# Moving the pieces of a projection to fixed steps in a graph attention kernel, and its first weights ahead of other work

## The chip, the cores and the metric

The kernel runs on one core of a Trainium2 chip. The metric is the device time of one execution in microseconds (us). The median of several runs counts, and a profile of one further execution tells where its time goes.

## What is computed

The program is a graph layer with attention, a graph convolution and two layer norms. Nearly all of its time goes into the attention, which is this part of the reference:

```python
q = (x @ Wq.T).reshape(d, n, h)
k = (x @ Wk.T).reshape(d, n, h)
v = (x @ Wv.T).reshape(d, n, h)
a = jnp.einsum('dnh,dmh->dnm', q, k) * scale
a = a + spatial_encoding + edge_encoding
a = jax.nn.softmax(a, axis=2)
out = jnp.einsum('dnm,dmh->dnh', a, v)
```

Here n = 2708, d = 128 and h = 8, and both encodings are the adjacency matrix `adj` (2708 x 2708). So there are 128 attention problems of 2708 x 2708 scores. All of them add the same matrix `adj` twice before the exponential. The reshape takes the projected rows in their flat order: problem d uses the values from d x 2708 x 8 on, which belong to a short run of rows of x. The projections of later rows of x are therefore needed only by later problems.

## The kernel before, in words

**Tiles.** Four problems make a group (`GB = 4`), so there are 32 groups. The 2708 queries of a group are cut into six blocks of 452 (the last has 448), and the 2708 keys into 21 chunks of 128 and a short one of 20. A block is worked through in nine steps, which gives 54 steps in a group and 1728 in all. A step takes two to four *pieces* of the scores, of two tiles of 128 keys x 452 queries each (tile `s` in PSUM, two buffers), and three more tiles of the chunk that the step treats in another way (tile `p` in PSUM, one buffer).

**One step on each engine.** TensorE makes the scores (L438). VectorE adds the adjacency to the two tiles of a piece and writes them to `e` (L445). ScalarE takes the exponential of the three tiles in `p` and writes `w` (L534), and GpSimd multiplies `w` with the exponential of the adjacency (L535). When all pieces of the step have been added, ScalarE takes the exponential of `e` in one instruction (L537). Later TensorE multiplies the weights in `e` and `w` with the values and adds up in `acc` (L455, L460, L463). At the end of a block VectorE copies `acc` out (L469). In the first group ScalarE also makes the exponentials of the adjacency (L418), which are stored to memory (L420) and read back in the later groups.

**The order of TensorE's work** is made by the generator `interleave` (L40 to L129) when the program is built. It keeps estimates of when each engine will be done, and yields one of four things: a piece of scores, an addition to `acc` (`add_up`), the copy of a finished block (`hand_on`), or a piece of a projection (`amid`). Each engine gets its instructions in the order in which the generator yields them. A projection piece comes ahead of the step's first piece of scores, and at which steps one comes is told by the list `amid` (L474). The assertion below that list holds a projection to being done before its group needs it.

**The projections.** The projections of the first two chunks of 128 rows of x are made whole, ahead of the attention (`project_all`, L377 to L406). Those of the other 20 chunks are cut into 240 pieces, 12 to a chunk: K, Q and V, four pieces each (`quarters`, L321). These are the pieces that the list `amid` places. One piece (`project`, L338) is a product of 128 rows with 256 columns of weights (L344, two instructions on TensorE, which use one of the two `s` buffers), a copy by VectorE (L346), for K and Q a split into two parts on GpSimd (L359, L360), two stores (L364), or one for V (L354), and the load of the next piece's weights (`load_quarter`, L329, with the DMA in L336). The copy goes with the product. The split, the stores and the load are put on the list `jobs`, and one job is taken from it in each step, ahead of its second piece of scores (L495): the split in the step of the projection, the stores in the next, the load in the one after that. For V the store comes in the same step and the load in the next. The tiles for the weights (`wc`), for the rows of x (`xc`) and for the copies have one buffer each.

**The DMA queue of SyncE (SP).** SP issues nearly all DMAs, in program order. At the start of a step it gets the loads of adjacency tiles for the steps ahead (`load_adj`, eight tiles ahead, L513), in the fourth step of a block those of the next queries (L500), and over a group those of the next group's keys and values (L505 to L511). Before the attention starts it gets, in this order: x and the weights for the first two chunks (L370, L373), two adjacency tiles (L375), the stores of the first chunk's K and Q, the loads of the first group's keys and queries, six more adjacency tiles, the values, the stores of the second chunk, and then the rows and weights for the first piece (`load_quarter(0)`, L407).

The functions around the change, with the lines that the profile names:

Of the kernel before, what the change touches and what calls it, by code (L numbers as in the profile page):

```python
# [142 lines left out]
def graph_attention_gcn(ctx: ExitStack, tc: tile.TileContext, x, xT, adj, adjT, adjP, adjS,  # L143
# [45 lines left out]
    with ExitStack() as s:  # L189
# [28 lines left out]
        for m in range(NU):  # L218
            if m not in TWO_EXP:
                pairs += [[(m, 0), (m, 1)], [(m, 2), (m, 3)]]  # L220
            elif left_over.index(m) % 2:
# [4 lines left out]
        plan = [(pairs[cuts[i] : cuts[i + 1]], m, [j for j in range(GB) if j != left_out[m]])  # L226
                for i, m in enumerate(TWO_EXP)]
# [62 lines left out]
        def load_adj(n):  # L290
            g, b, m = loads[n]
            n0, nw = QBS[b]
            if isinstance(m, tuple):
                t = adj_cols[g, b, m] = twos.tile([P, 2, QB], F32, tag="two", name="two")
                for i, x in enumerate(m):
                    nc.sync.dma_start(t[:, i, :nw], (adjS if x == NU else adjP[ds(x * P, P), :])[:, ds(n0, nw)])
            elif m < 0 and g > 0:
                t = exp_cols[g, b, -1 - m] = ecols.tile([P, QB], F32, tag="ecol", name="ecol")
                nc.sync.dma_start(t[:, :nw], near_exp[b, -1 - m][:, :nw])
            else:  # L300
                t = adj_cols[g, b, m] = cols.tile([P, QB], F32, tag="col", name="col")
                m = -1 - m if m < 0 else m
                nc.sync.dma_start(t[:, :nw], adjP[ds(m * P, P), ds(n0, nw)])
# [17 lines left out]
        quarters = [(c, i, h) for c in range(FIRST, NM) for i in range(3) for h in range(4)]  # L321
# [7 lines left out]
        def load_quarter(n):  # L329
            c, i, h = quarters[n]  # L330
            i0, mi = MC[c]
            if i == h == 0:
                given[c] = proj.tile([P, P], F32, tag="xc", name="xc")
                nc.sync.dma_start(given[c][:, :mi], xT[:, ds(i0, mi)])
            given[c, i, h] = proj.tile([P, QW], F32, tag="wc", name="wc")
            nc.sync.dma_start(given[c, i, h], projections[i][0][:, ts(h, QW)])  # L336
# [36 lines left out]
            nc.sync.dma_start(first_w[:, ds(2 * NB * i, 2 * NB)], w)  # L373
        for n in range(2):
            load_adj(n)  # L375

        def project_all(c, i):  # L377

            dst = projections[i][1]
            pp = ps.tile([P, 2, NB], F32, tag="s", name="s")  # L380
            for h in range(2):
                nc.tensor.matmul(pp[:, h, :], first_x[:, ts(c, P)], first_w[:, ts(2 * i + h, NB)], start=True, stop=True)
            o = flat(epool.tile([P, 8, QB], F32, tag="e", name="e"))[:, : 4 * NB].rearrange("p (l f) -> p l f", l=2)
            if i == 2:
                nc.scalar.copy(o[:, 0], flat(pp))
                return lambda: nc.sync.dma_start(dst.rearrange("(i g) e -> i (g e)", g=P)[ts(c, P)], o[:, 0])
            f = half_scale if i == 1 else 1.0
            nc.scalar.mul(o[:, 0].bitcast(F32R), flat(pp), f)
            nc.vector.scalar_tensor_tensor(o[:, 1].bitcast(F32R), flat(pp), f, o[:, 0], ALU.mult, ALU.subtract)
            return lambda: nc.sync.dma_start(dst.rearrange("r (i g) -> i r g", g=P)[ts(c, P)],  # L390
                                             o.rearrange("p l (e g) -> p (l e) g", g=P))
# [12 lines left out]
            load_values(0, j)  # L404
        for i in range(3):
            project_all(1, i)()  # L406
        load_quarter(0)  # L407
        for h in range(9):
            order_keys(0, h, (nc.gpsimd.tensor_copy, nc.vector.tensor_copy, nc.scalar.copy)[h % 3])
        for j in range(GB):  # L410
# [60 lines left out]
                nc.sync.dma_start(os_[:, ds((GB * g + j) * N + n0, nw)], o[ds(32 * j, H + 1), :nw])  # L471

        where = {}
        amid = [2 + 32 * n // 5 for n in range(len(quarters))]  # L474
        for g in range(1, NG):
            c = (min(NG, g + 2) * GB * N - 1) // (P * P)
            assert c < FIRST or amid[quarters.index((c, 2, 3))] + 8 < 54 * g
# [375 lines left out]
```

## Time and profile before

| what | value |
|---|---|
| median of 3 runs | 6884.85 us (6881.82 to 6886.79) |
| the profiled execution's own time | 6884.26 us |
| its span in the profile | 6882.5 us |
| ScalarE, exponential of `e` (L537) | 1728 instructions, mean 2658 ns |
| ScalarE, exponential of `w` (L534) | 1728 instructions, mean 1323 ns |
| VectorE, addition of adjacency (L445) | 5568 instructions, mean 1.09 us |
| GpSimd, product (L535) | 1728 instructions, mean 3102 ns |
| projection piece on TensorE (L344) | 480 instructions, mean 428 ns |
| projection piece on VectorE (L346) | 240 instructions, mean 418 ns |
| projection piece on GpSimd (L359, L360) | 160 each, about 402 and 736 ns |
| DMA | 1674 MB, mean 243 GB/s |

The profile is of one execution. Times in it are counted from the start of its span, and its span is 1.8 us shorter than the execution's own time. A row of the waits view names an engine and line, what ended its wait, the total in us, how often, and the longest. A row of the timeline has the start and the length in us, the engine, the line, the operation, the tiles it writes and reads, and how many like instructions were put together in it (`x2`). In square brackets stands how long the engine had been idle and what ended that. Durations of instructions that follow each other on one engine may overlap in the record.

### The profile page before, as it was taken

What the parts mean: (1) busy time and instruction counts of PE and PEld (TensorE: products, weight loads), DVE (VectorE), ACT (ScalarE), POOL (GpSimd) and SP (SyncE); (2) the same over time, 40 slices, a digit from 0 to 9 for tenths busy, and PEclk for the clock granted to TensorE, in tenths of its full rate; (3) what the DMA queues carried; (4) which work ended last, traced back from release to release, by engine and by line L of the source; (5) the groups of instructions that cost most, each with busy time, mean ns of one, the idle gap of its engine ahead of it and who ended that gap; (6) DMA issues with size and microseconds to landing.
All of it is one profiled execution on the core that took longest, in us unless ns stands there. A gap on an engine that the chain in (4) does not pass through costs nothing.

```text
span 6882.5 us, 138849 instructions
## 1 busy us (share of the span) xinstructions
PE 6655.3 (97%) x50666; PEld 2002.7 (29%) x50666; DVE 6106.7 (89%) x6373; ACT 6505.4 (95%) x3659; POOL 5789.3 (84%) x2706
## 2 busy tenths in 40 slices
PE   7999999999999999999999999999999999999979
PEld 2222222222222222222222222222222222222254
DVE  6899999999999999999999999999999999999941
ACT  7999999999999999999999999999999999999910
POOL 5899988989888899998889999889898898888800
PEclk8999999999999999999999999999999999999999
DMA  8888888778888877788887778887788878777667
GB/s 254 261 250 250 249 244 248 243 246 250 249 254 245 239 245 244 246 251 252 246 243 248 244 240 250 242 253 243 248 251 247 249 233 239 243 233 230 193 204 233
DMA packets 1168590, 1674.27 MB, mean 243 GB/s; under 512 B 153982, under 2 KB 1135954, under 8 KB 1163802
## 3 DMA queue, kind: packets, MB, share of 16 engines
q1 hardware_dynamic: 1167642, 1664.50, 79.0%
q8 instruction: 402, 6.59, 0.4%
q14 instruction: 290, 2.38, 0.1%
q10 hardware_dynamic: 256, 0.81, 0.1%
HBM read 1582.90 MB, written 81.80 MB: 242 GB/s over the span
## 4 chain that ended last, share of the span: by engine, by line
PE 58%; DMA 11%; DVE 11%; POOL 6%; issue 5%; ACT 5%; SPq 4%; DVEq 0%; ACTq 0%; POOLq 0%
PE acc L463 29%; PE s L438 18%; DVE e L445 10%; POOL w L535 6%; DMA col<-in_adjP 4%; PE acc L680 3%; DMA two<-in_adjP 3%; ACT e L537 3%; PE p L438 2%; PE acc L455 2%; SPq L287 2%; ACT w L534 2%; DMA ecol<-ne 2%; PE s L344 1%; PE acc L460 1%
## 5 line engine op out<-in xcount | busy, mean ns | idle before, releaser
L535 POOL TENSOR_TENSOR w<-w,ecol 128x1356 f32<-128x1356 f32 (+1 forms) x1728 | 5347.8, 3102 | 696.1 <-ACT w L534 601.6
L445 DVE TENSOR_TENSOR e<-s,col 128x904 f32<-128x904 f32 (+1 forms) x4608 | 4817.2, 1091 | 320.6 <-PE s L438 130.3
L537 ACT ACTIVATE e<-e 128x2712 f32<-128x2712 f32 (+5 forms) x1728 | 4593.8, 2658 | 9.3 <-DVE e L445 4.3
L463 PE MATMUL acc<-e,vals 128*9 128x452 f32 x20352 | 3561.9, 545 | 0.4 <-ACT e L537 0.4
L438 PE MATMUL s<-q,k 32*128 32x452 f32 x10944 | 2475.2, 462 | 120.9 <-DVE e L445 93.3
L534 ACT ACTIVATE w<-p 128x1356 f32<-128x1356 f32 (+1 forms) x1728 | 2286.0, 1323 | 33.9 <-PE p L438 20.4
L438 PEld LDWEIGHTS s<-q,k 32*128 32x128 f32 x10944 | 997.6, 182 | 3267.6 <-DVE e L445 2845.5
L463 PE MATMUL acc<-w,vals 128*9 128x452 f32 x10368 | 1622.0, 544 | 0.0
L438 PE MATMUL p<-q,k 32*128 32x452 f32 (+1 forms) x5184 | 1328.1, 444 | 21.2 <-ACT w L534 19.6
L445 DVE TENSOR_TENSOR e<-s,two 128x904 f32<-128x904 f32 (+1 forms) x960 | 1048.3, 1092 | 126.5 <-PE s L438 81.3
L463 PEld LDWEIGHTS acc<-e,vals 128*9 128x9 f32 x20352 | 441.7, 88 | 786.2 <-issue 773.7
L438 PEld LDWEIGHTS p<-q,k 32*128 32x128 f32 x5184 | 547.1, 182 | 51.0 <-ACT w L534 45.3
L463 PEld LDWEIGHTS acc<-w,vals 128*9 128x9 f32 x10368 | 207.0, 88 | 175.8 <-issue 160.3
L262 POOL CAST k<-k_raw 128x336 fp32r<-128x336 f32 x251 | 222.2, 886 | 30.1 <-DMA q<-qs 30.1
L460 PE MATMUL acc<-e,v_first 128*32 128x452 f32 (+1 forms) x1536 | 188.9, 564 | 9.8 <-DVE o L469 2.0
L455 PE MATMUL acc<-e,v_short 128*128 128x452 f32 (+1 forms) x384 | 195.1, 590 | 0.0
L344 PE MATMUL s<-wc,xc 128*128 128x256 f32 (+1 forms) x480 | 166.4, 428 | 8.9 <-DMA wc<-in_WkT 7.5
L469 DVE COPY o<-acc 128x452 f32<-128x452 f32 x192 | 119.9, 624 | 40.0 <-PE acc L463 39.8
L360 POOL TENSOR_TENSOR pr<-pa,pr 128x256 fp32r<-128x256 f32 (+1 forms) x160 | 117.8, 736 | 12.8
L346 DVE TENSOR_SCALAR pa<-s 128x256 f32<-128x256 f32 (+1 forms) x240 | 100.2, 418 | 27.6 <-PE s L344 23.9
L344 PEld LDWEIGHTS s<-wc,xc 128*128 128x128 f32 (+1 forms) x480 | 70.5, 184 | 133.4 <-DVE e L445 116.4
L680 PE MATMUL acc<-col,xw 128*128 128x512 f32 (+2 forms) x264 | 106.0, 551 | 0.0
(85 smaller groups left out, 1041.6 us busy)
## 6 DMA issues: line engine op xcount, KB each, us to landing
col<-in_adjP SPq DMA_DIRECT2D x1965, 226.0 KB
two<-in_adjP SPq DMA_DIRECT2D x1440, 226.0 KB
ecol<-ne SPq DMA_DIRECT2D x1395, 226.0 KB
col<-in_adjP SPq DMA_DIRECT2D x393, 224.0 KB
two<-in_adjP SPq DMA_DIRECT2D x288, 224.0 KB
ecol<-ne SPq DMA_DIRECT2D x279, 224.0 KB
col<-in_adjT SPq DMA_DIRECT2D x210, 256.0 KB
k_raw<-ks SPq DMA_DIRECT2D x504, 84.6 KB
```

Source lines behind the costliest of these rows:

```text
L262: copy(k[:, :, ts(i, n)], t[:, ts(i, n * NU)].rearrange("p (q c) -> p c q", c=NU))
L287: queues[i].dma_start(q[ds(32 * j + 2 * H * i, 2 * H), :nw].bitcast(F32), qs[:, ds((GB * g + j) * N + n0, nw)])
L344: nc.tensor.matmul(pp[:mi, 0, :QW], given[c][:, :mi], given.pop((c, i, h)), start=True, stop=True)
L438: nc.tensor.matmul(to[:, :nw], k[r, m, :], q[r], start=True, stop=True)
L445: nc.vector.tensor_add(e[:, ds(at, 2), :nw], st[:, :, :nw], a)
L455: nc.tensor.matmul(a[:, :nw], vz, e[:, t, :nw], start=False, stop=False)
L460: nc.tensor.matmul(a[ds(32 * j, 32), :nw], v_first[g % 2][:, ds(32 * j, 32)], e[:, t, :nw], start=True, stop=False)
L463: nc.tensor.matmul(a[ds(32 * j, VW), :nw], v[:, m, ds(VW * j, VW)], e[:, t, :nw], start=False, stop=(m == last_chunk))
L534: nc.scalar.activation(w[:, :, :nw], sp[:, :, :nw], AF.Exp, scale=2.0)
L535: nc.gpsimd.tensor_mul(w[:, :, :nw], w[:, :, :nw], exp_cols[g, b, two][:, :nw].unsqueeze(1).to_broadcast([P, 3, nw]))
L537: nc.scalar.activation(e[:, :at, :nw], e[:, :at, :nw], AF.Exp, scale=2.0)
L680: nc.tensor.matmul(acc[:, :nw], src[:mw, m, :], t[:mw, :nw], start=(m == 0), stop=(last is None and m == NM - 1))
```

## The change

The first piece's rows and weights are loaded right behind the first two adjacency tiles, no longer behind the work on the second chunk. The list of the steps that a projection piece is put in front of is another one. Before, piece n (from 0) stood in front of step 2 + 32n // 5, that is one in 6.4 steps, at changing steps of a block. Now three pieces stand in every 18 steps (two blocks), always in front of steps 1 and 8 of the first block and of step 4 of the second. The pattern begins with its second place: the first piece stands in front of step 8, the next ones in front of steps 13, 19, 26, 31 and so on. The last piece, which stood in front of step 1531, now stands in front of step 1441. The number of pieces and what each does stay the same.

```diff
         for n in range(2):
             load_adj(n)
+        load_quarter(0)
 
         def project_all(c, i):
...
         for i in range(3):
             project_all(1, i)()
-        load_quarter(0)
         for h in range(9):
...
         where = {}
-        amid = [2 + 32 * n // 5 for n in range(len(quarters))]
+
+        assert len(plan) == 9
+        amid = [18 * (n // 3) + (1, 8, 13)[n % 3] for n in range(1, len(quarters) + 1)]
         for g in range(1, NG):
```

## What was predicted, and from what

> **What bounds the kernel now.** I read the page's busy times first.
>
> ```profile
> PE 6655.3 (97%) x50666; PEld 2002.7 (29%) x50666; DVE 6106.7 (89%) x6373; ACT 6505.4 (95%) x3659; POOL 5789.3 (84%) x2706
> ```
>
> TensorE looks busiest, but its matmuls overlap in the record, so I asked which engine never rests while the attention runs. It runs from about 44 to 6540 us, and ScalarE's exponentials (L534 on the product scores `w`, L537 on the added scores `e`) are due once in each of its 1728 steps. ScalarE's waits from 244 to 5840 us, where pieces of projections (L344) stand between the steps, are:
>
> ```profile
> ACT w L534 <- PE p L438: 17.6, 40, 0.8
> ACT e L537 <- DVE e L445: 3.3, 12, 0.6
> ACT w L534 <- PE s L438: 1.2, 4, 0.4
> ACT w L534 <- POOL w L535: 0.8, 1, 0.8
> ```
>
> That is 22.9 us of rest in 5596 us: ScalarE is the bound, and the other engines' waits are slack. An edit that leaves ScalarE's work alone can only win back its delays. To size them I read the timeline of ScalarE at the first L534 of groups 1, 27, 28 and 31 (54 steps a group; the last piece stands before step 1531, group 28).
>
> ```profile
> 283.10 1.36 ACT L534 ACTIVATE w<-p 128x1356 f32<-128x1356 f32 x1
> ...
> 5529.98 1.29 ACT L534 ACTIVATE w<-p 128x1356 f32<-128x1356 f32 x1
> ...
> 5731.72 1.30 ACT L534 ACTIVATE w<-p 128x1356 f32<-128x1356 f32 x1 [0.73 <-PE p L438]
> ...
> 6332.94 1.29 ACT L534 ACTIVATE w<-p 128x1356 f32<-128x1356 f32 x1
> ```
>
> A group with pieces takes (5529.98 - 283.10)/26 = 201.80 us, one without (almost) (6332.94 - 5731.72)/3 = 200.41. The pieces cost 1.40 us a group, 0.166 us for each of some 8.44. So all of them together cost about 38 us; that is what a better place can win at most, apart from the start. At the start the timeline shows this:
>
> ```profile
> 49.34 1.18 SPq L334 DMA_DIRECT2D xc<-in_xT  x1
> 50.57 1.24 SPq L336 DMA_DIRECT2D wc<-in_WkT  x1
> ...
> 53.28 0.19 ACT L418 ACTIVATION_READ_ACCUMULATOR ecol<-col 128x1 f32 x1
> ...
> 54.91 1.19 PE L344 MATMUL s<-wc,xc 128*128 128x256 f32 x2 [7.48 <-DMA wc<-in_WkT]
> ...
> 61.45 1.30 ACT L534 ACTIVATE w<-p 128x1356 f32<-128x1356 f32 x1 [7.98 <-PE s L438]
> ```
>
> The first piece stands before step 2; TensorE waits 7.48 us for its weights, and ScalarE, which needs step 2's scores from behind it, stands still for 7.98 us.
>
> **What the Trainium skill says.** "Perfetto Trace Analysis", Identifying the Most-Contended Engine, says that occupancy names the contended engine, except that matmul occupancy does not; the trace agrees, with ScalarE at rest for 0.4% of the middle. The same page, Optimizing Scalar/DVE Operations, says that half of a ScalarE instruction's own overhead, in the record, overlaps the next one; here L534 lasts 1.30 us and the next L537 starts 1.18 us after it. So I count from start to start. "PSUM — Partial Sum Buffer", Engine vs sequencer instructions, says that matmuls keep program order and the other queues are strict FIFO; the stall above agrees: what stands behind the piece waited 7.5 us with it. "DMA: Bandwidth & Descriptors", Anatomy of one DMA, says that waits are made by the issuing sequencer and prices a transfer at 2.0 us + bytes/436e3, for the 131 KB of weights an estimate of 2.3 us; here it was 4.3 us (50.57 to 54.88), behind three stores. I use 4.3.
>
> **The change part by part.** Nothing is added or removed: 240 pieces before and after, each two PE instructions, one DVE copy, two POOL instructions (not for V), its stores and one load. SP's queue has as many rows. What changes is where they stand.
>
> (1) *The first load, ahead of the second chunk's work.* SP issues xc and wc behind the adjacency loads, after 3.8 us; SP has nothing to issue from there to 11.19, so they cost nothing there. Every DMA waits for the one eight places before it on its semaphore; two more loads use two more of the eight, but those that come around have landed, and the key reads keep their pace. Behind the second chunk's stores two issues fall away, and the loads for steps 3 and 4 move ahead from 51.98 to 49.34, by 2.6 us.
>
> (2) *The first piece goes from step 2 to step 8*, for which the weights are there. Step 2's scores then need the p bank, free at 51.31 when L534 of step 1 ends (50.03 + 1.28); an e buffer, free when the store issued at 44.00 has been read (the same store at 11.19 had landed by 16.50, so 5.3 us, 49.3); and adjacency loaded long before. So ScalarE goes on at 53.47: up to 7.98 us won. What is late next is step 3's adjacency: issued until about 51.0 and landed by 55.3 (with 4.3 us), while the last add of step 3 has to start by 57.7 (L534 and L537 of step 2 and L418 and L534 of step 3 from 53.47 make 58.8, less 1.09 for the add). That fits by 2.4 us, on transfers that are busy with the stores. The piece's other instructions (VectorE's copy 0.42, POOL's 1.14, two stores and the next load on SP) leave steps 2 to 4 for steps 8 to 10, where the places of (3) price them. Bounds 5.0 and 8.0; I take 7.5.
>
> (3) *The places after that.* I write a piece's place as its step in the block of 9. Before, 2 + 6.4n (rounded down) visits all nine evenly. For each step I took the time from its L534 to the next step's L534 over what is usual for this step of the block (its 30th percentile, so the noise floor is near nothing), and summed over a piece's six steps, from the one before it to four after. Mean over 25 or 26 pieces at places 0 to 8: 0.55, 0.02, 0.02, 0.25, 0.26, 0.16, 0.22, 0.39, 0.39 us; mean 0.25. The new places 1, 8, 4 look like (0.02 + 0.39 + 0.26)/3 = 0.22, little better. But the planner also orders the work around a piece, so I ran its plain Python for both lists and took the order alone, no time, from it. After, the order repeats every 18 steps. Of these, 16 have steps in the trace before with the same order from two steps ahead to three behind (11 to 31 cases each), and the other two (next block, steps 1 and 2) over a narrower stretch. Their mean delays, summed: the piece at place 8 costs 0.39 (0.37 of it at the next block's first step, which has four adds), the one at place 4, in its new order, 0.09 and 0.06 at step 7, the one at place 1 0.01, the rest 0.02: 0.57 us in 18 steps. The trace shows the two costly ones:
>
> ```profile
> 4076.22 0.41 DVE L346 TENSOR_SCALAR pa<-s 128x256 f32<-128x256 f32 x1
> 4077.42 2.10 DVE L445 TENSOR_TENSOR e<-s,col 128x904 f32<-128x904 f32 x2 [0.79 <-ACT w L534]
> ...
> 4083.40 1.36 ACT L534 ACTIVATE w<-p 128x1344 f32<-128x1344 f32 x1
> 4084.93 3.19 ACT L537 ACTIVATE e<-e 128x3584 f32<-128x3584 f32 x1 [0.17 <-DVE e L445]
> ```
>
> Place 8: VectorE copies the piece, stands still, then adds without rest, and is late at the block's first step: L537 starts 1.53 us after L534, not 1.18.
>
> ```profile
> 3622.86 0.70 PE L344 MATMUL s<-wc,xc 128*128 128x256 f32 x2
> ...
> 3628.84 2.50 ACT L537 ACTIVATE e<-e 128x2712 f32<-128x2712 f32 x1
> 3631.27 1.30 ACT L534 ACTIVATE w<-p 128x1356 f32<-128x1356 f32 x1
> ```
>
> Place 4: the next L534 starts 2.43 us after L537, not 2.35. Filling every step from 54 to 1673 in this way gives 47.6 us of delay after; the same steps had 60.2 before (2.1 a group; 0.75 where no piece stands). Won: 12.6 us. The bound from below is places 8 and 4 at their plain means, (0.02 + 0.39 + 0.26) + 0.03 = 0.70 a period, 0.13 more in 77 periods, 10 us: 2.6 won. From above, if the stall at place 8 was only half as long, 80 x 0.19 = 15 more: 27. Likely 9 to 16.
>
> (4) *The queues passed.* SP: the weights for the piece at place 4 are issued two steps after the piece at place 8 and are due three steps later. Before, the 27 such loads were issued 4.1 us ahead of that step's L534 in the median (0.6 behind it at worst) and landed 3.8 us later; they are due 5.05 us behind it. Cover: 5.3 us; a gap of five steps instead of six eats 3.5 of what there was. POOL: a split (0.40 + 0.74) now falls on fixed steps of the group, some beside the key copies (0.89); POOL's product ended at most 6.8 us after its L534's start, against 4.5 usual, and is added up later than that. Both at nothing.
>
> **Sum.** From the profiled execution's own 6884.26 us (span 6882.5 and 1.8 around it; the median of the runs is 6884.85): 6884.26 - 7.5 - 12.6 = 6864.2 us.
>
> **Rivals.** 0.2%, 13.8 us, is about what a measurement of this kernel can tell from no change: 6871.1 to 6898.6 counts as the same.
> *B, the start gives nothing:* behind the stores the transfers are the bound, and ScalarE waits at steps 3 to 5 instead of step 2. For it: the issues of SP at 44 to 52 us are slow (1.2 to 3.1 us). Against it: 2.4 us of slack and far more bytes an us later. Then 6884.26 - 12.6 = 6871.7.
> *C, slower, the weights at place 4 late:* if SP is as late at that load as it is before step 3 of a block (3.4 us behind L534), they land at 3.4 + 3.8 = 7.2, and are due at 5.05: TensorE waits 2.2 us in each of 80 periods, all of it on ScalarE: 6864 + 172 = 7036. It decides from a lateness of 1.2 us on. Against it: none of the 27 was so late.
> *D, more won:* the piece at place 8 always stands seven steps behind the one before it, so VectorE may have recovered and the delay may go: 80 x 0.39 = 31 less, 6833. Against it: the 20 like cases cost 0.26 to 0.75 each.
>
> **Chances.** Forecast 0.80, B 0.10, C 0.05, D 0.05. The forecast alone spans 6857 (start 8.0, places 19) to 6871, and the range goes to 6873 to hold B. Faster by over 0.2%: 0.84 (D, and nearly all of the forecast); within: 0.11; slower: 0.05.
>
> **What would show it.** Right: no L344 row before 60 us and L534 of step 2 at about 53.5 without idle time; ScalarE's first L534 of groups 1 and 27 about 201.4 us a group apart (199.66 without any delay, and three times 0.57); the delays at the first step of every second block, about 0.37 us each. Wrong: ScalarE waiting for adjacency or adds between 55 and 70 us (2); PE L344 idle before it on DMA wc (4); delays at other steps of the 18 (3).

## The result, and the profile after

The changed kernel takes 6870.08 us (median of 16 runs, 6864.01 to 6881.51) against 6886.35 before (16 runs). The ratio is 0.9977, with a 95% interval of 0.9970 to 0.9984: some 16 us faster, between 11 and 21. The forecast was 20 us, 6864.2. The profiled execution took 6865.95 us, with a span of 6863.4.

The page's busy times of the changed kernel:

```profile
PE 6632.4 (97%) x50666; PEld 1992.4 (29%) x50666; DVE 6109.7 (89%) x6373; ACT 6506.3 (95%) x3659; POOL 5788.8 (84%) x2706
```

The instruction counts are those of before, and the busy times of ScalarE (ACT), VectorE (DVE) and GpSimd (POOL) are the same to within 0.1%. So no work of these engines went; only waiting did. L534 and L537 of before are L536 and L539 now. These are all of ScalarE's waits in the changed kernel from 240 to 5840 us:

```profile
ACT e L539 <- DVE e L445: 11.1, 25, 0.7
ACT w L536 <- PE p L438: 1.0, 3, 0.3
```

It was 22.9 us in 57 waits, most of them on the product scores `p`. Now it is 12.1 us, nearly all on VectorE's adds. The first exponentials of groups 1, 27 and 31 in ScalarE's timeline give the time of a group:

```profile
276.75 1.50 ACT L536 ACTIVATE w<-p 128x1356 f32<-128x1356 f32 x1
...
5514.81 1.45 ACT L536 ACTIVATE w<-p 128x1356 f32<-128x1356 f32 x1
...
6317.17 1.29 ACT L536 ACTIVATE w<-p 128x1356 f32<-128x1356 f32 x1
```

(5514.81 - 276.75)/26 = 201.46 us a group, where it was 201.80; the four groups from 27 on, which have no pieces, take (6317.17 - 5514.81)/4 = 200.59. I took each step's delay as in the prediction, against the same usual times. It makes 50.7 us from step 54 to 1673, where it was 60.2.

**Where the 19.1 us between the two spans came from:** 6.3 us up to group 1's first exponential (283.10 to 276.75), 9.4 in steps 54 to 1673 and 4.5 in the last steps (7.5 to 3.0 us of delay), less 1.2 lost in the layers behind. Not all of this belongs to the change. Of the 6.3, 1.6 lie ahead of the first exponential, whose time varied between 39.7 and 46.5 us in the profiles below. The last steps cost 5.8 to 7.7 us in eleven of the twelve. One profile is one execution, and its parts have to be read next to those of other kernels with the same stretch.

### The profile page after: what moved, and what is told of

Read it like the earlier page. It is cut to its first block, busy times and chain, and to the rows that moved or that the text cites. A ratio compares the mean times of both kernels' runs of the same rounds, so it can differ in the third digit from the quotient of the medians.

```text
span 6863.4 us, 138873 instructions
## 1 busy us (share of the span) xinstructions
PE 6632.4 (97%) x50666; PEld 1992.4 (29%) x50666; DVE 6109.7 (89%) x6373; ACT 6506.3 (95%) x3659; POOL 5788.8 (84%) x2706
## 4 chain that ended last, share of the span: by engine, by line
PE 52%; DMA 12%; DVE 11%; POOL 7%; issue 7%; ACT 6%; SPq 5%; DVEq 0%; POOLq 0%; ACTq 0%
PE acc L463 26%; PE s L438 16%; DVE e L445 9%; POOL w L537 6%; DMA col<-in_adjP 4%; DMA two<-in_adjP 3%; SPq L287 3%; PE acc L682 3%; ACT e L539 3%; ACT w L536 2%; DMA ecol<-ne 2%; PE acc L455 2%; PE p L438 2%; PE s L344 1%; DMA two<-in_adjS 1%
## 5 line engine op out<-in xcount | busy, mean ns | idle before, releaser
L537 POOL TENSOR_TENSOR w<-w,ecol 128x1356 f32<-128x1356 f32 (+1 forms) x1728 | 5347.5, 3102 | 678.8 <-ACT w L536 598.4
L539 ACT ACTIVATE e<-e 128x2712 f32<-128x2712 f32 (+5 forms) x1728 | 4616.5, 2672 | 17.6 <-DVE e L445 12.0
L536 ACT ACTIVATE w<-p 128x1356 f32<-128x1356 f32 (+1 forms) x1728 | 2308.2, 1336 | 3.0 <-PE p L438 2.5
```

The source lines that it names most:

```text
L536: nc.scalar.activation(w[:, :, :nw], sp[:, :, :nw], AF.Exp, scale=2.0)
L537: nc.gpsimd.tensor_mul(w[:, :, :nw], w[:, :, :nw], exp_cols[g, b, two][:, :nw].unsqueeze(1).to_broadcast([P, 3, nw]))
L539: nc.scalar.activation(e[:, :at, :nw], e[:, :at, :nw], AF.Exp, scale=2.0)
```

## Experiments

Twelve kernels ran. Each ratio is against the kernel before on the same chip; the changed kernel's is 0.9977. In the diffs `-` is the changed kernel unless another is named.

### Which part of the change does it: the load, the places, the start

*The load alone* (the changed kernel with the old list):

```diff
-        amid = [18 * (n // 3) + (1, 8, 13)[n % 3] for n in range(1, len(quarters) + 1)]
+        amid = [2 + 32 * n // 5 for n in range(len(quarters))]
```

> The first piece's weights are loaded ahead of the second chunk's work, the pieces stay at their old steps (the first at step 2). Theory: the change wins 6 us at the start, where TensorE no longer waits for weights, and 9 us by the places after that; so this kernel wins about 6 us, 6880 against 6886 before, and ScalarE's delays in groups 1 to 29 stay at 60 us. Rival 1, the start makes all of it: 6870. Rival 2, the places make all of it: 6886.

Measured: 6886.44 us, ratio 0.9999 (0.9991 to 1.0007). The load alone wins nothing that can be told. TensorE's wait for weights is gone, but ScalarE's 8 us of rest at step 2 come back in parts over steps 1 to 8. All stalls in the first 12 steps make 8.2 us here, 9.2 before. The delay of steps 54 to 1673 is 4.7 us above that of before, with the same list; two profiles can lie that far apart.

*The places alone* (the kernel before with the new list):

```diff
-        amid = [2 + 32 * n // 5 for n in range(len(quarters))]
+        amid = [18 * (n // 3) + (1, 8, 13)[n % 3] for n in range(1, len(quarters) + 1)]
```

> The new places, with the first piece's weights loaded where they were, behind the second chunk's stores. Theory: the places win their 9 us; at the start step 2 no longer waits, but the loads for steps 3 to 5 stand behind the two extra issues (2.4 us), so only 3 to 4 us are won there: 6873. Rival 1, the early load makes all of it: 6886. Rival 2, the places make all of it and the load's place is worth nothing: 6870.

Measured: 6866.43 us, ratio 0.9976 (0.9969 to 0.9982). That is the whole effect, as rival 2 had it. The profile has 44.5 us of delay in steps 54 to 1673.

*The new start with the old rest:*

```diff
         amid = [18 * (n // 3) + (1, 8, 13)[n % 3] for n in range(1, len(quarters) + 1)]
+        amid[15:] = [2 + 32 * n // 5 for n in range(15, len(quarters))]
```

> Early load, the first 15 pieces at the new places and the other 225 at the old ones. Theory: the start's 6 us and some 0.6 us for group 1, nothing after that: 6879, with ScalarE's delays in groups 2 to 29 as before (58 us). Rival, the gain is in the start alone: 6870.

Measured: 6883.74 us, ratio 0.9999 (0.9991 to 1.0007), and 59.0 us of delay. Load and first piece together are worth about 2 us by the medians, which this measurement can't tell from nothing; its interval reaches to 6 us won, not to 7.5. The first 12 steps' stalls are 6.9 us. The theory's 6 us at the start fell here.

### What took the start's gain

In the changed kernel, step 2 no longer waits, as predicted. Here are ScalarE's exponentials of `w` in steps 2 and 3, and the exponential of adjacency that opens step 5:

```profile
52.00 1.30 ACT L536 ACTIVATE w<-p 128x1356 f32<-128x1356 f32 x1 [0.15 <-PE s L438]
...
56.47 1.28 ACT L536 ACTIVATE w<-p 128x1356 f32<-128x1356 f32 x1
...
66.51 0.58 ACT L418 ACTIVATE ecol<-col 128x452 f32<-128x452 f32 x1 [2.29 <-DMA col<-in_adjP]
```

And this is SP's timeline ahead of that wait:

```profile
58.72 5.04 SPq L287 DMA_DIRECT2D q<-qs  x8
63.86 0.37 SPq L303 DMA_DIRECT2D col<-in_adjP  x1
```

The adjacency for step 5 is issued behind eight loads of queries, which hold SP for 5 us. Before, TensorE's 7.5 us of waiting had hidden them. To see whether SP's order or the transfers are the bound, I issued these queries later:

```diff
-                if i == 3 and nq[0] < NG:
+                if i == (3 if n > 9 else 7) and nq[0] < NG:
```

> The changed kernel, in which the loads of the second block's queries, in the first block alone, are issued in step 7 and not in step 3. Theory: of the 9.4 us won at step 2 the profile shows 3 given back at steps 3 to 6, where ScalarE waits for adjacency that SP issued behind eight loads of queries (5 us of SP); without them there the start wins 2 to 3 us more: 6867. Rival, the transfers and not SP's order are the bound there: 6870, with the wait at step 5 as it is.

Measured: 6867.93 us, ratio 0.9969 (0.9958 to 0.9979). The interval overlaps the changed kernel's, so a gain in time isn't shown. That the wait at step 5 goes is shown: the same exponential starts without one.

```profile
59.31 0.58 ACT L418 ACTIVATE ecol<-col 128x452 f32<-128x452 f32 x1 [1.19 <-DMA col<-in_adjP]
...
65.42 1.30 ACT L536 ACTIVATE w<-p 128x1356 f32<-128x1356 f32 x1 [1.32 <-PE s L438]
...
68.98 0.58 ACT L418 ACTIVATE ecol<-col 128x452 f32<-128x452 f32 x1
```

What stays are 1.2 us at step 3, on adjacency, and 1.3 at step 4. So the queries in front of step 5's tiles cost what stood there; the rest is left to the transfers behind the second chunk's stores, which was not tested by itself. The stalls of the first 12 steps are 4.5 us with this edit. With the changed kernel's start as it is they were 4.8, 6.9, 8.0 and 6.5 us in four profiles (the changed kernel, the new start with the old rest, and the two with the copy twice, below), 6.5 in the mean, with 0.7 to 2.3 us of waiting at step 5. But over all 54 steps of the first group the delay is 36.7 us, and 34.6, 36.9, 37.8 and 36.5 in those four (30.5 of each are the extra exponentials): what the edit wins by step 12 it loses again by step 54.

### What a piece in front of step 8 costs, and why

Mean delay of ScalarE at some of the 18 steps (us), from groups 1 to 25. The steps are counted from 0; the pieces stand in front of steps 1, 8 and 13, and steps 9 and 13 are the first and the fifth of the second block. "The planner" is the generator `interleave`.

| kernel | step 1 | step 9 | step 13 | all 18 |
|---|---|---|---|---|
| changed | 0.01 | 0.38 | 0.09 | 0.62 |
| VectorE's copy twice at step 8 | 0.01 | 0.36 | 0.08 | 0.58 |
| VectorE's copy twice at step 1 | 0.20 | 0.45 | 0.10 | 0.87 |
| no engine's work in any piece | 0.00 | 0.29 | 0.00 | 0.44 |
| planner not told of step 8 | 0.01 | 0.06 | 0.59 | 0.81 |
| the same, no engine's work at step 8 | 0.00 | 0.00 | 0.02 | 0.20 |

*VectorE's copy twice*, in front of step 8 and, in another kernel, of step 1 (with `== 1`):

```diff
-            nc.vector.tensor_scalar_mul(a, pp[:mi, 0, :QW], half_scale if i == 1 else 1.0)
+            for _ in range(2 if amid[n] % 9 == 8 else 1):
+                nc.vector.tensor_scalar_mul(a, pp[:mi, 0, :QW], half_scale if i == 1 else 1.0)
```

> The changed kernel, in which VectorE makes its copy of the piece twice where the piece stands in front of step 8 of a block (80 pieces, 0.42 us each). Theory: the 0.38 us that ScalarE loses at the next block's first step come of VectorE being late there, so each second copy is paid in full: 80 x 0.42 = 34 us, 6904, with 0.8 us at that step. Rival: the product's time on TensorE makes the delay, VectorE has slack: 6870.

Measured: 6866.79 us, ratio 0.9976 (0.9967 to 0.9985). Nothing is paid.

> The changed kernel, in which VectorE makes its copy of the piece twice where the piece stands in front of step 1 of a block (80 pieces, 0.42 us each). Theory: VectorE has slack there (the piece costs ScalarE 0.01 us), so nothing or little is paid: 6870 to 6874. Rival, each us of VectorE counts wherever it stands: 6870 + 34 = 6904.

Measured: 6890.51 us, ratio 1.0007 (1.0000 to 1.0014), some 21 us more than the changed kernel, or 0.26 us for each of 80 second copies. ScalarE's waits from 300 to 5500 us, first with the second copy at step 8, then at step 1:

```profile
ACT e L540 <- DVE e L446: 9.6, 22, 0.7
```

```profile
ACT e L540 <- DVE e L446: 20.0, 73, 0.7
```

Both forecasts were wrong, and the wrong way round. VectorE has slack at step 8 and little at step 1. A likely reason, not tested: step 1 has only two pieces, so ScalarE comes back for VectorE's sums soonest there.

*The pieces without engines.* Products, copies and splits are left out, and zeros are stored; so keys, queries and values of all but the first 256 rows of x are zero.

```diff
-            pp = ps.tile([P, 2, NB], F32, tag="s", name="s")
-            nc.tensor.matmul(pp[:mi, 0, :QW], given[c][:, :mi], given.pop((c, i, h)), start=True, stop=True)
-            a = proj.tile([P, QW], F32, tag="pa", name="pa")[:mi]
-            nc.vector.tensor_scalar_mul(a, pp[:mi, 0, :QW], half_scale if i == 1 else 1.0)
+            a = blank_a[:mi]
...
-            o = proj.tile([P, 2, QW], F32R, tag="pr", name="pr")[:mi]
+            o = blank_o[:mi]
...
-                nc.gpsimd.tensor_copy(o[:, 0], a)
-                nc.gpsimd.tensor_sub(o[:, 1], a, o[:, 0].bitcast(F32))
+                pass
```

> The changed kernel without the 240 pieces' products on TensorE, copies on VectorE and splits on GpSimd: their stores write zeros, so that keys, queries and values of all rows of x but the first 256 are zero; loads and stores stay. Theory: the pieces' delays come of the engines' order, so all but the steps' own 0.75 us a group goes, 30 us: 6840. Rival, the pieces' DMAs on SP's queue make the delays: 6870.

Measured: 6862.84 us, ratio 0.9964 (0.9950 to 0.9977), with 40.7 us of delay. I expected 20. Three quarters of the delay at step 9 is still there without any engine's work in a piece: the order alone is enough to make it. (The pieces' loads and stores stay here. They stay in the next two kernels as well, which lose 0.06 us and nothing at step 9.) TensorE's timeline of this kernel at step 8, and ScalarE's exponential of step 7:

```profile
2251.32 0.48 PE L439 MATMUL p<-q,k 32*128 32x452 f32 x3 [0.83 <-ACT w L537]
```

```profile
2249.92 1.34 ACT L537 ACTIVATE w<-p 128x1356 f32<-128x1356 f32 x1
```

TensorE waits 0.83 us for ScalarE to be done with step 7's `p` (2249.92 + 1.34 = 2251.26), since the planner has put product scores of step 8 right behind its first piece of scores. It had reckoned with the projection piece ahead of them. The scores behind wait too, and VectorE starts the next adds late. In the changed kernel the same order costs the time in another way. At the same step of the same group TensorE and VectorE show:

```profile
2250.09 0.70 PE L344 MATMUL s<-wc,xc 128*128 128x256 f32 x2
2250.72 0.55 PE L463 MATMUL acc<-e,vals 128*9 128x452 f32 x1
...
2251.60 0.47 PE L438 MATMUL s<-q,k 32*128 32x452 f32 x2
2251.88 0.48 PE L438 MATMUL p<-q,k 32*128 32x452 f32 x3
```

```profile
2250.93 0.41 DVE L346 TENSOR_SCALAR pa<-s 128x256 f32<-128x256 f32 x1
2252.17 2.11 DVE L445 TENSOR_TENSOR e<-s,col 128x904 f32<-128x904 f32 x2 [0.82 <-ACT w L536]
```

Between the piece's product and the step's first scores the planner has put an addition to `acc` (eight matmuls, from 2250.72 on). So the first scores start 1.5 us behind the product, and VectorE, done with its copy at 2251.34, rests 0.82 us until they are there: its add starts 0.10 us behind their end (2251.60 + 0.47 = 2252.07). It is so at all 75 steps of this kind in groups 1 to 25. The view puts the rest down to ScalarE's `w`, but step 7's exponential had ended 0.34 us earlier (2250.49 + 1.34 = 2251.83 in ScalarE's timeline). With the copy twice the same rest is 0.36 us long, and there the view names TensorE's scores: the second copy fits into the rest, which is why it cost nothing. The product scores do wait for step 7's exponential here, until 2251.88, but the adds behind follow without a gap. At the next block's first step ScalarE has four adds to wait for:

```profile
2258.32 1.35 ACT L536 ACTIVATE w<-p 128x1344 f32<-128x1344 f32 x1
2259.74 3.20 ACT L539 ACTIVATE e<-e 128x3584 f32<-128x3584 f32 x1
```

1.42 us from start to start and not 1.18.

*The planner not told of step 8.* If the order makes the delay, another order must take it away:

```diff
+        told = [n for n in amid if n % 9 != 8]
...
-        for what, n, c, beside in interleave(plan, len(steps) // len(plan), NU, amid, bufs=5):
+        for what, n, c, beside in interleave(plan, len(steps) // len(plan), NU, told, bufs=5):
...
             nw = QBS[b][1]
+            if c == 0 and n in amid and n not in told:
+                jobs += project(amid.index(n))
```

> The changed kernel, in which the planner is not told of the 80 pieces in front of step 8, which are put in ahead of that step's first scores all the same. New theory: the delay at the next block's first step (0.37 us) comes of the order that the planner makes around the piece, with step 8's three product scores behind its first piece of scores, where TensorE has to wait until ScalarE has emptied the p bank of step 7; without the piece in its reckoning the planner puts them behind the third. Then 80 x 0.29 = 23 us go (0.09 us was the work's own share), about 6845, and the delay at that step is under 0.1 us. Rival, the piece's own work makes the delay whatever the order: 6868.

Measured: 6883.42 us, ratio 0.9997 (0.9988 to 1.0005): the whole gain of the change is lost. The delay at step 9 does go, from 0.38 to 0.06 us. In this order the first scores come ahead of the addition to `acc`, as soon as VectorE has emptied their buffer:

```profile
2261.87 0.70 PE L344 MATMUL s<-wc,xc 128*128 128x256 f32 x2
2262.85 0.48 PE L438 MATMUL s<-q,k 32*128 32x452 f32 x2 [0.28 <-DVE e L445]
```

VectorE rests 0.29 us here and not 0.82. So with the piece's work in place another order takes the delay away. It moves two things, the first scores ahead of the addition and the product scores behind the third piece. Which of them counts is not tested by itself; the theory above names the second, and the changed kernel's trace speaks for the first.

But step 13, with the piece at place 4, now costs 0.59. ScalarE's timeline at steps 9 and 13 to 14:

```profile
2270.10 1.35 ACT L539 ACTIVATE w<-p 128x1344 f32<-128x1344 f32 x1
2271.27 3.26 ACT L542 ACTIVATE e<-e 128x3584 f32<-128x3584 f32 x1
...
2285.31 2.53 ACT L542 ACTIVATE e<-e 128x2688 f32<-128x2688 f32 x1
2288.27 1.29 ACT L539 ACTIVATE w<-p 128x1344 f32<-128x1344 f32 x1 [0.43 <-PE p L438]
```

At step 9 the second exponential follows after 1.17 us; at step 14 the first follows 2.96 us after the one before it, not 2.34. It waits for the product scores. Either the order at place 4 is bad by itself now, or the piece at place 8 had set TensorE and VectorE back and they have not caught up five steps later. I took away that piece's work in this kernel (its product, copy and split; a third of the projected values becomes zero):

```diff
+            empty = amid[n] % 9 == 8
+            a = blank_a[:mi]
+            if not empty:
...
-            o = proj.tile([P, 2, QW], F32R, tag="pr", name="pr")[:mi]
+            o = blank_o[:mi] if empty else proj.tile([P, 2, QW], F32R, tag="pr", name="pr")[:mi]
```

> The kernel of e9_planner_not_told_of_8, whose pieces in front of step 8 have no product, copy and split (their stores write zeros; loads and stores stay), so that a third of the projected values is zero. In e9 the delay at the next block's first step went from 0.37 to 0.06 us, but the piece at place 4, five steps after the one at place 8, cost 0.59 us at its own step and not 0.08. Theory: TensorE and VectorE make up for a piece over several steps, a stall of ScalarE is one way in which they catch up, and so the setback of the piece at place 8 is only handed on to place 4. Then without its work step 13 is back at 0.1 us, 80 x 0.5 = 40 us less than e9: 6843. Rival: the order at place 4 costs 0.5 us by itself once the planner is not told of place 8: 6883 as e9.

Measured: 6838.22 us, ratio 0.9930 (0.9916 to 0.9943). Step 13 is back at 0.02 us. ScalarE's timeline at the same place:

```profile
2267.53 2.57 ACT L551 ACTIVATE e<-e 128x2688 f32<-128x2688 f32 x1
2269.87 1.42 ACT L548 ACTIVATE w<-p 128x1344 f32<-128x1344 f32 x1
```

2.34 us. So it was the setback, handed on: a piece that costs ScalarE next to nothing at its own place still puts the others back, and that is paid where the next piece comes. It is not the pieces' loads and stores either, which are all still there. In the changed kernel step 13 costs only 0.09 us, though the planner's order is the same in both kernels from the second piece of scores of step 10 on. That the stall of ScalarE at step 9 is what lets TensorE and VectorE catch up there fits this, but was not tested by itself.

*The planner told of no piece at all* (`told = []` in the kernel above):

> The changed kernel, in which the planner is told of no piece at all, so that the order of scores and sums is that of a kernel without pieces, and every piece is put in ahead of its step's first scores. New theory, as a stronger form: the steps' own 0.75 us a group stays (20 us), and the work of the pieces at places 8 and 4 adds 0.1 us each: 20 + 16 = 36 us of delay against 48, 6856. Rival: with no room left for the pieces TensorE and VectorE are late for several steps after each: 6870 or more.

Measured: 6921.48 us, ratio 1.0048 (1.0034 to 1.0062), with 1.32 us of delay in 18 steps: 0.70 at step 1, and 0.15, 0.12 and 0.23 at steps 9, 12 and 14. The rival was right; the planner's room for pieces is needed.

### Other places

*Places 1, 0 and 5* (steps 1, 9 and 14 of 18):

```diff
-        amid = [18 * (n // 3) + (1, 8, 13)[n % 3] for n in range(1, len(quarters) + 1)]
+        amid = [18 * (n // 3) + (1, 9, 14)[n % 3] for n in range(1, len(quarters) + 1)]
```

> The changed kernel with other places: three pieces in 18 steps, in front of steps 1 of the first block and 0 and 5 of the second. Theory: the delay of a piece is set by the order around it, and the orders of this kernel have all been seen in the traces of before and after; their mean delays make 31.5 us from step 54 to 1673 against 50 in the changed kernel: 18 us less, 6852. Rival, the delay depends on what came in the steps before as well, or the five steps between pieces leave the weights late: 6870 or more.

Measured: 6854.57 us, ratio 0.9957 (0.9943 to 0.9970), with 35.2 us of delay. It is the fastest kernel here that computes everything, about 14 us better than the changed one at the centres of the two intervals, which just touch. The reading of the orders was off by 4 us.

*Places 1, 5 and 5, with two buffers:*

```diff
-        amid = [18 * (n // 3) + (1, 8, 13)[n % 3] for n in range(1, len(quarters) + 1)]
+        amid = [18 * (n // 3) + (1, 5, 14)[n % 3] for n in range(1, len(quarters) + 1)]
...
-                if n + 1 < len(quarters):
-                    load_quarter(n + 1)
+                if n + 2 < len(quarters):
+                    load_quarter(n + 2)
```

(with `bufs=2` for `xc` and `wc`, `load_quarter(1)` behind `load_quarter(0)`, and the later queries)

> Places in front of step 1 and step 5 of the first block and of step 5 of the second, with two buffers for the pieces' rows and weights, so that a load is issued one piece earlier, and the second block's queries loaded later in the first block. Theory (delays are those of the order): the orders seen so far make 17 us of delay from step 54 to 1673 against 48: 31 us less than the changed kernel, 6838. Rival, four steps between two pieces are too few for VectorE and GpSimd, or the weights are late: 6855 or more.

Measured: 6876.84 us, ratio 0.9988 (0.9981 to 0.9995), with 58.1 us of delay against an expected 17. The piece at step 5, four steps behind the one at step 1, costs 0.51 us at step 4; the one at step 14, nine steps behind, costs 0.01 at step 13. The orders of the two are alike from four steps ahead on. What differs is that the first has a piece right ahead of that stretch. The weights were not late: no wait of TensorE for them shows in this profile. The run changes places, buffers and queries at once, so their shares are not told apart.

## Why the prediction was right or wrong

**What bounds the kernel: right.** ScalarE's work stayed, and what was won came out of its delays. The ceiling of 38 us, 200.41 us a group, is about what the best order seen comes to: with two thirds of the pieces' work and the planner not told of step 8 a group takes 200.25 us. But the delays belong to the orders as much as to the pieces: without any piece's work, in the order made for them, 40.7 of the 50.7 us stay.

**(1) and (2), the start: the mechanism right, the size wrong.** Step 2 went on at 52.00 with 0.15 us of rest in place of 8 (53.47 was forecast; all is 1.6 us earlier in this profile). The term "I take 7.5" was mis-sized: in the profiles the stalls of the first 12 steps fell from 9.2 to 6.5 us in the mean of four, so 2.7 us were won, and the timed kernel with the new start and the old rest shows about 2 us that are not clear of nothing. The step that failed is that the account ends at step 3, with "That fits by 2.4 us". It reckons with 4.3 us for a load, from the issue of the first weights at 50.57 to their landing at 54.88. Step 3 itself waited only 0.23 us in the changed kernel. But I did not follow SP's queue on to step 5, whose tiles stand behind eight loads of queries, and ScalarE waited 2.29 us there. The sign named for this, ScalarE waiting for adjacency between 55 and 70 us, came. It is rival B in the main, but not by the transfers alone: about 2 of the missing us went when the queries were moved. The range's lower bound, 5.0, was too high. The gain came within 4 us of the forecast one all the same, as the places were the larger term.

**(3), the places: right in size.** The delays of steps 54 to 1673 should have gone from 60.2 to 47.6 us. They are 50.7 in the changed kernel and 44.5, 47.4 and 48.3 in three others with the same places and no other work that costs ScalarE (the places alone, the copy twice at step 8, the queries later), 47.7 in the mean, which is 12.5 won. Also right by step: 0.38 at step 9 (0.37 foreseen), 0.09 at step 13 and 0.06 at step 16. With 2.7 for the start the sum is 15.2 us, against 16 measured. The changed kernel's own profile has 9.5 for the places, and 4.5 in the last steps that no term foresaw.

**Place 8: the sequence right, its cause not given.** I wrote that VectorE copies the piece, stands still, then adds without rest and is late, and so it does. What it stands still for I did not say. The theory of the kernel with the copy twice, that VectorE's time counts there, was wrong. The next one, the wait for `p`, holds for the kernel without the pieces' work; in the changed kernel VectorE's rest ends with the first scores, which stand behind an addition to `acc`. Both come of the planner's order. The number stood all the same, because it was read from steps with that order, whatever its cause.

**(4), the queues: right.** In the changed kernel TensorE waited for a piece's weights once, at the fifth piece, which stands at place 4:

```profile
PE s L344 <- DMA wc<-in_WqT: 0.2, 1, 0.2
```

Rival C did not come. Nor did D: the piece at place 8 still costs 0.38 us at step 9. The kernel whose planner is not told of it shows that nothing is won where this delay alone goes.

**What the look-up of orders missed.** It takes a step's delay as set by the order from two steps ahead to three behind. For the changed kernel this held within 3 us, for places 1, 0 and 5 within 4. For places 1, 5 and 5, with four steps between two pieces, it failed by 41 us. And in the kernel whose planner is not told of step 8, step 13 has the order of the changed kernel over that whole stretch, five steps behind a piece, and cost 0.59 us and not 0.09.

**Open.** It is open how much of the last steps' 4.5 us belongs to the change: two profiles with the same end had 3.0 and 5.8. Which part of the order around a piece at place 8 makes the delay is open too. So is whether the later queries are worth having, which their interval does not tell. That the transfers are what holds steps 3 and 4 at the start is read from the waits; it was not tested by itself.

## What to carry to other kernels

Find the engine that never rests, and price an edit by that engine's delays, from start to start and step by step; like steps elsewhere in the same trace give a first price of a new order before it runs. But a delay is not always paid where its cause stands: engines with little slack can hand a setback on, so a stall taken away may come back dearer at the next disturbance. And where one wait at the start is taken away, follow the in-order load queue some steps further: what that wait had hidden may be what comes late next. Where the profile names what ended a wait, compare the times: an engine that was done 0.34 us before is not it.

## What was not expected

The planner's order costs 0.29 us at step 9 with no piece's work there at all, while the same work in another order costs 0.06. And paying the 0.38 us is cheaper than not: in the kernel without it the next piece costs 0.59.
